# Four strided transfers for the first adjacency block, four-block stores and three transfers for the attention rows

## The chip, the cores and the metric

One core of a Trainium2 chip runs the kernel. The metric is device time in microseconds (us), median over runs. "Partition" is a row of the on-chip memory (128 of them); "queue" is the order in which one engine issues its transfers; the 16 DMA engines of the core carry out what all queues issue.

## The reference, cut to what matters

```
def reference(x, adj, W, a):              # x 4096x512, adj 4096x4096, W 512x2048, a 4x1024x1, all f32
    ht = (x @ W).reshape(N, 4, 512).transpose(1, 0, 2)
    src = einsum('hnd,hd->hn', ht, a[:, :512, 0])
    dst = einsum('hnd,hd->hn', ht, a[:, 512:, 0])
    e = leaky_relu(src[:, :, None] + dst[:, None, :], 0.01) + adj[None]
    h = einsum('hij,hjd->hid', softmax(e, axis=-1), ht).mean(axis=0)
    return layernorm(x + h, axis=-1)
```

The entries of adj are zero or as large as 1e9, while the attention scores are small. The softmax of a row is therefore, with the data at hand, all on the column where adj is largest. The kernel uses this: it finds that column for each row, gathers that row of x, multiplies it by the mean of the four heads' W, adds x and normalises. It also computes a bound that says whether this short form holds for all rows; if it doesn't, a general path (`general`) follows. With the inputs given it isn't entered.

## The kernel before

The 4096 rows are split into 32 blocks of 128. Partition p of block ib holds row p*32 + ib, so neighbouring partitions of one block are 32 rows of adj apart in main memory (32 rows x 16 KB = 512 KB), and one partition's neighbouring blocks are neighbours in main memory. A block of adj is 128 rows of 16 KB, 2 MB.

The function `leading_rows` is one hand-written order of instructions (`manual_schedule`): each engine takes its own in program order.

- SyncE (SP) issues all large transfers in one queue. Ahead of the loop stand: adj of block 0 (L132, through `load_adj`, L119 to L124), W in two halves of 2 MB (L130) with adj of blocks 1 and 2 after each, adj of blocks 3 and 4, and x of blocks 0 to 3 (L143). In the loop over t = 0 to 31 (L432) it issues adj of block t + 5 and, at a few t, more of x. The last blocks' adj come in 2 or 4 pieces of columns. After the loop come all the stores (L491 to L496, L551 to L553).
- ScalarE (ACT) issues the rows of `a` in four transfers of two rows of 2 KB (L133 to L137), then works on evictions, squares and normalisations.
- VectorE (DVE) reduces each block of adj to maxima of short segments (L180), finds the leading segment (L187, L189), and, two blocks later, the column in it (L223). The first reduction of block 0 waits for the whole of that block.
- GpSimd (POOL) issues the two gathers of each block, the leading segment (L200) and the row of x (L211), in a queue of its own.
- TensorE (PE) transposes the gathered rows (L238) and multiplies them by the mean of W (L253).

Six buffers hold adj. A new block is issued when the reduction of the block six before has freed its buffer.

Transfers issued by SP and ACT share eight completion semaphores, given out in turn; before a semaphore is used again the issuing queue waits for the transfer that used it last. A later transfer can therefore be held until the one eight before it has landed, beside what its own data need.

The output of block ib takes the place of x of that block in the tile `hold`. `store` (L337) writes n neighbouring blocks: each partition writes n x 2 KB in one run, 4 KB for two blocks, 8 KB for four. Before the change, blocks 0 to 7 are stored by fours (L491), 8 to 15 by twos (L493), 16 to 23 by fours (L495), and the last eight by twos and ones.

Of the kernel before, what the change touches and what calls it, by code (L numbers as in the profile page):

```python
# [9 lines left out]
F32 = mybir.dt.float32  # L10
# [10 lines left out]
P = 128  # L21
# [9 lines left out]
def gat_resnorm_kernel(  # L31
# [29 lines left out]
    any_bad = keep.tile([1, 1], I32, name="any_bad")  # L61

    leading_rows(tc, x, adj, W, a, out, ident, v, n_bad, any_bad)

    flag = nc.values_load(any_bad[0:1, 0:1], min_val=0, max_val=N)
# [5 lines left out]
def leading_rows(ctx, tc, x, adj, W, a, out, ident, v, n_bad, any_bad):  # L71
# [8 lines left out]
    nc = tc.nc  # L80
    N, D = x.shape
    H = a.shape[0]
    KB, NB = D // P, N // P
    AHEAD = 5
    Q = 4
    PIECES = 4
    LATE = NB - Q
    BEHIND = LATE - Q

    once = ctx.enter_context(tc.tile_pool(name="once", bufs=1))  # L90
    adj_pool = ctx.enter_context(tc.tile_pool(name="adj_pool", bufs=AHEAD + 1))
# [7 lines left out]
    adj_rows = adj.rearrange("(p nb) m -> nb p m", nb=NB)  # L99
# [11 lines left out]
    a_rows = once.tile([2 * H, D], F32, name="a_rows")  # L111

    once.tile([P, 32], F32, name="pad_end")
    adj_t = {}

    def pieces(ib):
        return PIECES if ib == NB - 1 else 2 if ib >= LATE else 1

    def load_adj(ib):  # L119
        if 0 <= ib < NB:  # L120
            t = adj_t[ib] = adj_pool.tile([P, N], F32, name="adj_t")
            n = pieces(ib)
            for k in range(n):
                nc.sync.dma_start(t[:, ts(k, N // n)], adj_rows[ib][:, ts(k, N // n)])  # L124
# [4 lines left out]
    def load_w(kb, n):  # L129
        nc.sync.dma_start(hold[:, ds(w_at + kb * H, n * H), :], w_blocks[:, ds(kb * H, n * H), :])  # L130

    load_adj(0)  # L132
    for s in range(2):  # L133
        for h in range(0, H, H // 2):
            nc.scalar.dma_start(
                a_rows[ds(s * H + h, H // 2), :], a[ds(h, H // 2), ts(s, D), :].rearrange("h d o -> h (d o)")
            )  # L137
    for kb in range(0, KB, 2):
        load_w(kb, 2)
        load_adj(kb // 2 + 1)  # L140
# [196 lines left out]
    def store(queue, lo, n):  # L337
        queue.dma_start(out_rows[:, ds(lo, n), :], hold[:, ds(lo, n), :])
# [93 lines left out]
    for t in range(NB):  # L432
# [29 lines left out]
        ib = t - PROJECT  # L462
# [25 lines left out]
    for ib in range(BEHIND, LATE):  # L488
        row_norm(ib)
    nc.scalar.activation(xx, xx, AF.Sqrt)  # L490
    for ib in range(0, 2 * Q, Q):  # L491
        store(nc.sync, ib, Q)
    for ib in range(2 * Q, 4 * Q, 2):  # L493
        store(nc.sync, ib, 2)
    for ib in range(4 * Q, BEHIND, Q):  # L495
        store(nc.sync, ib, Q)  # L496
    add_x(nc.gpsimd, BEHIND)
    find_column(NB - 2)
# [208 lines left out]
```

## Time and profile before

| | |
|---|---|
| median of three runs | 235.25 us (235.2 to 236.05) |
| the profiled execution | 234.9 us |
| its span, first to last instruction | 233.4 us |
| moved by the DMA engines | 97.12 MB, mean 416 GB/s over the span |
| busy: PE, DVE, ACT, POOL | 86%, 82%, 48%, 43% |
| granted TensorE clock, mean | 0.965 |

The page splits the span into 40 slices of 5.8 us and gives for each the busy tenths of every engine, the DMA engines' busy share and the GB/s that they moved. A second view gives the same for any stretch that one names. A timeline lists the instructions of one engine with start and duration; for SP and ACT's transfers that is the time of issuing, not of moving data. Beneath these lie the trace's records of single packets: start, duration, size and queue. A packet is here one contiguous run on one DMA engine: 16 KB for a row of adj, 4 or 8 KB for a store, 2 KB for a row of `a`.

### The profile page before, as it was taken

The page shows a single profiled execution, that of the slowest core. Times are in us where ns is not written, and L with a number is a line of the kernel's source. Part 1 is how long each engine was busy: PE and PEld are TensorE (multiplying, and loading weights), DVE is VectorE, ACT ScalarE, POOL GpSimd, SP SyncE. Part 2 cuts the span into 40 slices and gives each one's busy share as a digit, 9 for nine tenths or more (in the row PEclk, how much of TensorE's full clock was granted, in tenths as well). Part 3 has the DMA queues.
Part 4 walks back from the last instruction along what each step waited for, and adds up shares of the span by engine and source line. Part 5 has one row for each costly group of instructions (what it writes and reads, how often), then busy time and mean ns, then how long its engine had stood idle before and what let it go on. Part 6 is the DMA issues. An engine that isn't in the chain of part 4 may idle for free.

```text
span 233.4 us, 2484 instructions
## 1 busy us (share of the span) xinstructions
PE 199.9 (86%) x683; PEld 105.3 (45%) x683; DVE 191.3 (82%) x300; ACT 111.8 (48%) x267; POOL 100.7 (43%) x215
## 2 busy tenths in 40 slices
PE   0069995999999999999999779879998977999980
PEld 0034644646565555665645244334443433444460
DVE  0548299689929999999788995999999999998881
ACT  2001223014474757575767455545664644188561
POOL 2020234414524464644543452647464564548300
PEclk9999999579999999999999979999999999999997
DMA  6999999999999999999999999999999999999995
GB/s 237 423 432 428 428 438 426 415 439 436 422 421 437 423 431 425 431 419 428 430 430 428 432 423 432 423 430 421 426 433 420 426 423 426 412 424 420 421 414 213
DMA packets 12257, 97.12 MB, mean 416 GB/s; under 512 B 1992, under 2 KB 2440, under 8 KB 6480
## 3 DMA queue, kind: packets, MB, share of 16 engines
q1 hardware_dynamic: 8640, 88.08, 89.1%
q0 software_dynamic: 3584, 8.84, 9.6%
q8 instruction: 6, 0.10, 0.2%
q14 instruction: 11, 0.09, 0.1%
q10 hardware_dynamic: 16, 0.02, 0.0%
HBM read 88.54 MB, written 8.39 MB: 415 GB/s over the span
## 4 chain that ended last, share of the span: by engine, by line
DMA 64%; DVE 21%; PE 11%; SPq 1%; issue 1%; ACT 0%; DVEq 0%
DMA adj_t<-in_adj_dram 53%; DVE seg L180 17%; DMA hold<-in_x_dram 11%; PE o L253 6%; PE o L295 2%; DVE at L189 1%; PE tp L238 1%; DVE top L187 1%; PE o L246 1%; DVE within L223 1%; SPq L130 1%; PE o L291 0%; SPq L124 0%; DVE inner L217 0%; ACT hold L335 0%
## 5 line engine op out<-in xcount | busy, mean ns | idle before, releaser
L180 DVE TENSOR_REDUCE seg<-adj_t 128x128 f32<-128x2048 f32 (+3 forms) x66 | 145.5, 2208 | 28.5 <-DMA adj_t<-in_adj_dram 28.2
L253 PE MATMUL o<-w_sum,yt 128*128 128x512 f32 x248 | 117.6, 616 | 0.7 <-ACT yt L240 0.7
L253 PEld LDWEIGHTS o<-w_sum,yt 128*128 128x128 f32 x248 | 45.6, 196 | 55.2 <-issue 43.9
L240 ACT COPY yt<-tp 128x512 f32<-128x512 f32 x32 | 18.8, 588 | 43.9 <-PE tp L238 43.8
L200 POOL DMA_INDIRECT lead<-in_adj_dram,row x32 | 32.3, 1008 | 14.6 <-POOL row L196 14.6
L211 POOL DMA_INDIRECT y<-in_x_dram,col x32 | 30.9, 964 | 15.4 <-POOL col L225 15.1
L238 PE MATMUL tp<-ident,y 128*128 128x128 f32 x128 | 22.1, 296 | 10.2 <-DMA y<-in_x_dram,col 10.1
L246 PE MATMUL o<-hold,ident 128*128 128x512 f32 x52 | 28.5, 634 | 1.7 <-DMA hold<-in_x_dram 1.7
L343 PE MATMUL o<-hold,ident 128*128 128x512 f32 x32 | 17.3, 696 | 13.6 <-DMA hold<-in_L_gnn_W_dram 13.6
L238 PEld LDWEIGHTS tp<-ident,y 128*128 128x128 f32 x128 | 18.5, 209 | 22.8 <-issue 20.5
L361 ACT COPY wt<-tp 128x512 f32<-128x512 f32 x16 | 9.2, 587 | 38.2 <-PE tp L359 38.2
L196 POOL TENSOR_TENSOR row<-at,first 128x1 uint32<-128x1 uint32 x32 | 6.1, 190 | 43.6 <-DVE at L189 43.6
L367 PEld LDWEIGHTS pv<-at_d,wt 128*128 128x128 f32 x128 | 17.2, 200 | 7.4 <-ACT wt L361 3.7
L260 ACT ACTIVATE sq<-hold 128x512 f32<-128x512 f32 x32 | 19.8, 620 | 0.0
L225 POOL TENSOR_TENSOR col<-start,within 128x1 uint32<-128x1 uint32 x31 | 5.9, 190 | 32.2 <-DVE within L223 32.2
L286 ACT ACTIVATE hold<-o,nm,sd 128x512 f32<-128x512 f32 x24 | 17.2, 771 | 0.0
L277 ACT ACTIVATE sq<-o,nm 128x512 f32<-128x512 f32 x24 | 16.5, 687 | 0.8
L343 PEld LDWEIGHTS o<-hold,ident 128*128 128x128 f32 x32 | 6.9, 225 | 21.5 <-issue 21.5
L367 PE MATMUL pv<-at_d,wt 128*128 128x2 f32 x128 | 16.0, 249 | 0.6 <-ACT wt L361 0.6
L344 ACT ACTIVATE w_sum<-o 128x512 f32<-128x512 f32 x4 | 2.4, 598 | 27.5 <-PE o L343 27.5
L275 ACT ACTIVATE sq<-o 128x512 f32<-128x512 f32 x24 | 14.5, 606 | 0.0
L187 DVE MAX8 top<-seg 128x8 f32<-128x256 f32 (+2 forms) x32 | 11.6, 362 | 1.1
(86 smaller groups left out, 140.0 us busy)
## 6 DMA issues: line engine op xcount, KB each, us to landing
adj_t<-in_adj_dram SPq DMA_DIRECT2D x28, 2048.0 KB, 30.8
adj_t<-in_adj_dram SPq DMA_DIRECT2D x6, 1024.0 KB, 28.1
hold<-in_L_gnn_W_dram SPq DMA_DIRECT2D x2, 2048.0 KB, 16.4
hold<-in_x_dram SPq DMA_DIRECT2D x2, 2048.0 KB, 37.6
out_dram<-hold SPq DMA_DIRECT2D x4, 1024.0 KB, 16.1
out_dram<-hold SPq DMA_DIRECT2D x7, 512.0 KB, 14.4
hold<-in_x_dram SPq DMA_DIRECT2D x3, 1024.0 KB
adj_t<-in_adj_dram SPq DMA_DIRECT2D x4, 512.0 KB, 19.8
```

Of the source, the lines that this page charges most:

```text
L180: nc.vector.tensor_reduce(seg_of[ib][:, ts(k, N // e // n)], adj_t[ib][:, ts(k, N // n)].rearrange("p (s e) -> p s e", e=e), axis=AX.X, op ...
L200: nc.gpsimd.indirect_dma_start(out=lead, out_offset=None, in_=adj_segs[e], in_offset=bass.IndirectOffsetOnAxis(ap=row[:, :1], axis=0),)
L211: nc.gpsimd.indirect_dma_start(out=y, out_offset=None, in_=x, in_offset=bass.IndirectOffsetOnAxis(ap=col[:, :1], axis=0),)
L238: nc.tensor.transpose(tp[:, kb, :], y[:, ds(kb, P, KB)], ident)
L240: nc.scalar.copy(yt, tp)
L246: nc.tensor.matmul(o_ps[ib], ident, hold[:, ib, :], start=start, stop=False)
L253: nc.tensor.matmul(o_ps[ib], yt_of[ib][:, kb, :], w_sum[:, kb, :], start=(start and kb == 0), stop=(kb == KB - 1),)
L260: nc.scalar.activation(sq, hold[:, ib, :], AF.Square, accum_out=xx[:, ib : ib + 1])
L277: nc.scalar.activation(sq, o, AF.Square, bias=nm[:, i], accum_out=sd[:, i])
L286: nc.scalar.activation(hold[:, ib, :], o_ps.pop(ib), AF.Identity, bias=nm[:, i], scale=sd[:, i])
L343: nc.tensor.matmul(o, ident, hold[:, w_at + kb * H + h, :], start=(h == 0), stop=(h == H - 1))
L367: nc.tensor.matmul(pv[:, kb, h : 2 * H : H], wt[:, k, :], at_d[:, k, h : 2 * H : H], start=(k == 0), stop=(k == KB - 1),)
```

## The change

Block 0 of adj is issued in four transfers: partitions 0, 8, 16 and so on (16 rows), 4, 12, 20 and so on (16 rows), 2, 6, 10 and so on (32 rows), and all odd ones (64 rows). Together they are the same 128 rows. The rows of `a` come in one transfer of four rows and two of two. The stores of blocks 8 to 15 are two of four blocks in place of four of two. SP's transfers ahead of the loop grow by three, ACT's fall by one, and the stores fall by two, so the count of all transfers is the same and the semaphores of those between are two places further on in turn.

```diff
-    load_adj(0)
-    for s in range(2):
-        for h in range(0, H, H // 2):
-            nc.scalar.dma_start(
-                a_rows[ds(s * H + h, H // 2), :], a[ds(h, H // 2), ts(s, D), :].rearrange("h d o -> h (d o)")
-            )
+    adj_t[0] = adj_pool.tile([P, N], F32, name="adj_t")
+    for lo, step in ((0, 8), (4, 8), (2, 4), (1, 2)):
+        some = ds(lo, P // step, step)
+        nc.sync.dma_start(adj_t[0][some, :], adj_rows[0][some, :])
+    for s, h, n in ((0, 0, H), (1, 0, H // 2), (1, H // 2, H // 2)):
+        nc.scalar.dma_start(a_rows[ds(s * H + h, n), :], a[ds(h, n), ts(s, D), :].rearrange("h d o -> h (d o)"))
...
-    for ib in range(0, 2 * Q, Q):
-        store(nc.sync, ib, Q)
-    for ib in range(2 * Q, 4 * Q, 2):
-        store(nc.sync, ib, 2)
-    for ib in range(4 * Q, BEHIND, Q):
+    for ib in range(0, BEHIND, Q):
         store(nc.sync, ib, Q)
```

## The prediction

> **What bounds the kernel now.** I read the page's slices first. Between the first and the last slice the DMA engines are 90% busy or more in every one, at 412 to 439 GB/s; no other engine is that steady.
>
> ```profile
> span 233.4 us, 2484 instructions
> ...
> DMA  6999999999999999999999999999999999999995
> GB/s 237 423 432 428 428 438 426 415 439 436 422 421 437 423 431 425 431 419 428 430 430 428 432 423 432 423 430 421 426 433 420 426 423 426 412 424 420 421 414 213
> ...
> q1 hardware_dynamic: 8640, 88.08, 89.1%
> ```
>
> So the stream of transfers is the bound from end to end. Time can be won only by starting it sooner, making its packets cheaper, or shortening what follows its last packet. The start and the end come next, in the view by stretches (columns: PE, PEld, DVE, ACT and POOL busy with counts, clock, DMA share, GB/s; a packet's bytes count where it starts, so fine stretches jump).
>
> ```profile
> 1.75:2.00 0.25, 0.00 (x0) 0.00 (x0) 0.00 (x0) 0.00 (x0) 0.25 (x4) 1.00 0.40 82
> 2.00:2.25 0.25, 0.00 (x0) 0.00 (x0) 0.00 (x0) 0.00 (x0) 0.25 (x5) 1.00 0.99 197
> 2.25:2.50 0.25, 0.00 (x0) 0.00 (x0) 0.00 (x0) 0.00 (x0) 0.13 (x3) 1.00 0.22 66
> 2.50:2.75 0.25, 0.00 (x0) 0.00 (x0) 0.00 (x0) 0.17 (x1) 0.00 (x0) 1.00 0.77 197
> 2.75:3.00 0.25, 0.00 (x0) 0.00 (x0) 0.00 (x0) 0.25 (x1) 0.00 (x0) 1.00 1.81 524
> ...
> 229.00:230.00 1.00, 0.00 (x0) 0.00 (x0) 0.00 (x0) 0.00 (x0) 0.00 (x0) 1.00 0.77 305
> 230.00:231.00 1.00, 0.00 (x0) 0.00 (x0) 0.00 (x0) 0.00 (x0) 0.00 (x0) 0.92 0.73 283
> 231.00:232.00 1.00, 0.00 (x0) 0.00 (x0) 0.00 (x0) 0.00 (x0) 0.00 (x0) 0.50 0.13 49
> ```
>
> The engines come in one after another over 0.9 us. The packet records say it exactly: the 16 engines' first packets start between 1.99 and 2.89 (mean 2.59) and end between 3.30 and 3.96 (mean 3.62); from then on a 16 KB packet takes 0.61 us. At the end the engines are still full at 229 and run dry by 231.8. SP's timeline gives the issues at the start:
>
> ```profile
> 0.98 0.39 SPq L124 DMA_DIRECT2D adj_t<-in_adj_dram  x1
> 1.42 0.43 SPq L130 DMA_DIRECT2D hold<-in_L_gnn_W_dram  x1
> 1.89 0.43 SPq L124 DMA_DIRECT2D adj_t<-in_adj_dram  x1
> 2.36 0.76 SPq L130 DMA_DIRECT2D hold<-in_L_gnn_W_dram  x1
> 3.17 0.44 SPq L124 DMA_DIRECT2D adj_t<-in_adj_dram  x1
> ```
>
> The issue of 128 rows ends at 1.37, and the first packet moves 0.62 us later. That W's second issue takes 0.76 instead of 0.43 says that something behind the queue needs more than the 0.47 us between issues to digest 128 rows; I take it that the spread of 0.9 us is the same thing, the making of 128 rows' descriptors.
>
> **What the Trainium skill says.** "DMA: Bandwidth & Descriptors", section "Latency and other measured facts", puts the first byte of such a transfer at about 600 ns; the trace agrees with 0.62. The same page, "Why a DMA increments its semaphore by 16 and not by 1", says a transfer is spread over the largest number of engines up to 16 that divides its rows, so 16 rows should give each engine one; the trace has only 128-row ones and the two-row transfers of `a`. "SBUF — State Buffer", section "Door 1: The DMA port swizzle", derives the memory port from the partition number: bits 2 to 4 and bit 6. By it partitions 0, 8, 16 ... reach 8 of 16 ports and 4, 12, 20 ... the other 8, while the third and fourth transfers reach all. No transfer in this trace shows that. The first page's table also lists a loss for copies between main-memory tensors at a row pitch of 4 MiB (103 against 164 GB/s at 2 MiB), which is the pitch of every eighth row here; no row here has that pitch, and it was not measured for loads.
>
> **The change part by part.**
>
> *Block 0 in four.* The first part has 16 rows, an eighth of the descriptors: by proportion 0.9/8 = 0.11 us of spread. All engines should then start near 1.99 to 2.1. Its second part is issued at about 1.45 and can feed the engines 0.62 us after its issue ends, about 2.45, before the first packets end (2.9 at the earliest). Third and fourth follow 0.47 us apart with 2 and 4 packets per engine, 1.2 and 2.4 us of work, so the engines don't run dry. Upper bound of the gain: every first packet ends about 2.9 (start 1.99 plus the 0.9 us that the late starters' first packets take), against a mean of 3.62: 0.7. Middle: the four that start first, 1.99 to 2.19, take 1.2 to 1.5 us, three of them ending together at 3.30 to 3.35; were that a floor set by memory, all would end at 3.3, a gain of 0.3. Lower bound, before the ports are counted: none. I take 0.4. It passes to the end one for one: DVE waits for adj 28.2 us in all, 11 times, so its work shifts with the loads; PE's run to the end begins at 201.55 when x lands; and the last store goes out at 228.80 into a queue still holding about 1 us of packets.
>
> *What the extra issues cost.* Three more issues of about 0.47 us move W's first half from 1.42 to about 2.8 on SP and everything behind it likewise. Block 0 alone keeps the engines busy to 1.99 + 8 x 0.61 = 6.9, so W's descriptors are 4 us early still: nothing. The semaphores come two places further on, so adj of block 1 and the second half of W, which waited for nothing, now wait for a part of block 0 or for rows of `a`; SP's whole queue stands behind each. The parts land from about 3.5 to 8, the rows of `a` landed by 9.2, and block 0 with W's first half covers the engines to 11.8. Nothing again; were the cover gone, each late issue would show one for one. In the loop SP waits longest for DVE's buffers (86.9 us behind the segment reduction alone), which the two places don't alter. DVE's first reduction now needs four landings, some 0.1 us more at most; it has 4.2 us of waiting before block 1.
>
> *Rows of `a`.* ACT issues three instead of four, at 0.24 to 0.54 each: about 0.3 us less ahead of a table load at 2.58. ACT's first work is at 20.11 and the rows are read at 20.0: nothing.
>
> *Stores.* 512 packets of 4 KB become 256 of 8 KB, per engine 32 become 16. The packet records have 0.159 us for the one and 0.309 for the other: 32 x 0.159 - 16 x 0.309 = 0.14 us less; counted from start to start (0.155 and about 0.305) it is 0.08. I take 0.1, all of it on the path because the engines stay full up to 230. SP has two issues (2 x 0.33) less, beside 12 us of waiting for data between 210 and 222: nothing. These results were finished long before (ACT's last write of a block under 24 ends at 195.1, the first store goes out at 198.64), so joining them holds nothing back. Gathers of x run between the larger packets and may take 0.15 us more for each one that they wait for; PE takes the last gathered row up at 221.6, some 5 us after it came: hidden.
>
> Sum: 0.4 + 0.1 = 0.5 less. The profiled execution's 234.9 (233.4 of span and 1.5 around it) goes to 234.4; the median lies 0.35 above that execution, so 234.75 is forecast. 0.5%, about what a measurement of this kernel can tell from no change, is 1.18 us: faster is below 234.07, slower above 236.43.
>
> **The rivals.**
>
> *The first packets are late for another reason than descriptors.* For it: the three early ones that end together. Then only the stores gain: 235.15. Between this and the forecast nothing in the trace of before decides.
>
> *The strided parts run below full rate.* Mechanism: a part that reaches 8 ports with 16 engines moves at half rate. If the skill's map holds and each engine has one row, parts one and two take 1.22 us each instead of 0.61: 1.2 more, less 0.5: 235.95. Should the pitch cost as much again, they take a quarter of the rate: 2 x 1.83 = 3.7 more, 238.45. Should all four parts share ports at half rate because rows are dealt to engines in order, 8 x 0.61 = 4.9 more: 239.65. It decides the sign from the moment that it costs over 0.5 us, that is, block 0's parts one and two at less than about 70% of full rate. For it: the map. Against it: if engines follow partitions, as with whole blocks, eight engines take two rows of part one and the other eight begin with part two, and no port is shared; then the gain is halved, not lost.
>
> *A larger gain.* The slowest engine's first packet ends at 3.96; if the last engine at the end is the one that started last, it gains up to 3.96 - 2.9 = 1.06, with the stores 1.2: 234.05.
>
> *A wait from the shifted semaphores starves the stream.* Against it: the 8 us of cover at the start, and at the end the six stores in flight hold some 6 MB, over 13 us. If it came, an SP issue delay of 0.5 to 1 us: 235.5 or so.
>
> **How the numbers follow.** Forecast 0.48; first packets late for another reason 0.20; strided parts slow 0.22, half of it with the first two parts at half rate only; larger gain 0.06; starved stream 0.04. The range 234.1 to 236.6 leaves out the larger gain and the heavier half of the strided case, 0.17. Faster by over 0.5% needs the larger gain, or the upper bounds of both terms with the scatter of the runs: 0.10. Slower by over 0.5% needs the heavier strided case and a little scatter: 0.15. Within: 0.75.
>
> **What would show it.** Right: all first packets start by about 2.2 to 2.5, block 0's last part lands near 8.2 instead of 8.67, the DVE's first reduction starts with it, and the last store is issued about 0.4 earlier than 228.80. Wrong: 16 KB packets above 0.61 us before 5 us (ports or pitch), a reduction that starts at 8.67 or later, a stretch in which the DMA share falls below 0.9 between 10 and 229. If the stores' packets don't shrink to 0.309 us per 8 KB, that term is wrong.

## The result and the profile after

The changed kernel takes 237.53 us (median of six runs, 237.16 to 238.63) against 235.36 before (235.09 to 236.05): the ratio is 1.0099 with a 95% interval of 1.008 to 1.0119. The forecast was 234.75 with a range of 234.1 to 236.6. The change made the kernel 2.2 us slower, and the time lies outside the range.

The profiled execution has a span of 235.9 us (237.52 as a run). The page's slices are the first view, as before:

```profile
span 235.9 us, 2483 instructions
...
DMA  5999999999999999999999999999999999999985
GB/s 164 375 431 438 425 429 421 431 430 420 434 427 433 421 432 429 430 422 429 431 427 428 428 426 436 419 441 408 436 420 426 426 427 419 414 426 424 423 354 212
```

The stream still fills the engines, but the first two slices moved 164 and 375 GB/s where they moved 237 and 423: 121 GB/s x 5.9 us, some 0.7 MB less, which is 1.7 us of the stream. A second loss is in the last slice but one, 354 instead of 414. SP's timeline and the stretches show the first:

```profile
0.97 2.52 SPq L135 DMA_DIRECT2D adj_t<-in_adj_dram  x4
3.54 0.59 SPq L130 DMA_DIRECT2D hold<-in_L_gnn_W_dram  x1
```

```profile
2.00:4.00 2.00, 0.00 (x0) 0.00 (x0) 0.00 (x0) 1.28 (x1) 0.38 (x6) 1.00 0.76 219
4.00:6.00 2.00, 0.00 (x0) 0.00 (x0) 0.00 (x0) 0.00 (x0) 0.00 (x0) 1.00 0.95 272
6.00:8.00 2.00, 0.00 (x0) 0.00 (x0) 0.00 (x0) 0.00 (x0) 0.00 (x0) 1.00 0.96 328
8.00:10.00 2.00, 0.00 (x0) 0.00 (x0) 0.00 (x0) 0.00 (x0) 0.00 (x0) 1.00 0.97 377
10.00:12.00 2.00, 0.00 (x0) 0.00 (x0) 0.99 (x1) 0.00 (x0) 0.00 (x0) 1.00 1.05 451
```

Read the last two columns together. In the first row the engines stand idle for a part of the time (0.76, after an empty first half microsecond). From 4 to 10 us they are busy, 0.95 to 0.97, but move only 272 to 377 GB/s: their packets are slow. Before, the stretch from 2 to 4 us moved 287 GB/s, and the next three were these:

```profile
4.00:6.00 2.00, 0.00 (x0) 0.00 (x0) 0.00 (x0) 0.00 (x0) 0.00 (x0) 1.00 0.92 393
6.00:8.00 2.00, 0.00 (x0) 0.00 (x0) 0.00 (x0) 0.00 (x0) 0.00 (x0) 1.00 1.04 446
8.00:10.00 2.00, 0.00 (x0) 0.00 (x0) 1.33 (x1) 0.00 (x0) 0.00 (x0) 1.00 1.00 428
```

From 10 us on the rate is the old one. The packet records give the detail: the 16 first packets start between 2.39 and 3.32 instead of 1.99 and 2.89, and between 4 and 8 us single 16 KB packets take up to 2.44 us instead of 0.61. By 10 us the changed kernel has moved 2.33 MB where the old one had 3.06; the missing 0.73 MB are 1.7 us of the stream. Its engines have had packets under way for 7.20 us each instead of 7.63. So 0.4 of the 1.7 us is engines without work, more than half of it before 3.4 us, and 1.3 is packets that take longer. DVE's timeline shows the delay that this hands on:

```profile
11.01 4.48 DVE L180 TENSOR_REDUCE seg<-adj_t 128x128 f32<-128x2048 f32 x2 [11.01 <-DMA adj_t<-in_adj_dram]
```

The first reduction starts at 11.01 instead of 8.67, 2.3 us late. The last piece of adj is reduced 2.7 us later than before, and the span is 2.5 us longer. Beyond the start there is thus one more thing, which the end of the span shows:

```profile
226.00:228.00 2.00, 2.00 (x9) 1.23 (x8) 1.72 (x4) 1.82 (x3) 0.00 (x0) 1.00 0.86 356
228.00:230.00 2.00, 2.00 (x11) 1.76 (x10) 1.89 (x7) 1.96 (x5) 0.00 (x0) 1.00 0.74 295
230.00:232.00 2.00, 0.54 (x3) 0.14 (x1) 1.03 (x6) 0.29 (x1) 0.00 (x0) 1.00 0.81 332
```

The engines have gaps before the last results are stored: the stores are through, and the transfers wait for the computation. The last store goes out at 232.60, 3.8 us later than before, not 2.3.

### The profile page after: what moved, and what is told of

It reads as the page before. It is cut to its first block, busy times and chain, and to the rows that moved or that the text cites. A ratio compares the mean times of both kernels' runs of the same rounds, so it can differ in the third digit from the quotient of the medians.

```text
span 235.9 us, 2483 instructions
## 1 busy us (share of the span) xinstructions
PE 201.5 (85%) x683; PEld 106.1 (45%) x683; DVE 191.0 (81%) x300; ACT 111.7 (47%) x267; POOL 100.7 (43%) x215
## 4 chain that ended last, share of the span: by engine, by line
DMA 46%; POOL 18%; issue 17%; DVE 13%; PE 3%; ACT 0%; POOLq 0%; SPq 0%; DVEq 0%
DMA adj_t<-in_adj_dram 41%; DVE seg L180 9%; POOL lead L200 6%; POOL y L211 6%; DMA lead<-in_adj_dram,row 5%; POOL sd L281 2%; PE o L253 2%; PE o L295 2%; POOL row L196 1%; POOL start L207 1%; POOL col L225 1%; DVE col L231 1%; DVE at L189 1%; DVE top L187 1%; POOL sd L280 1%
## 5 line engine op out<-in xcount | busy, mean ns | idle before, releaser
L253 PE MATMUL o<-w_sum,yt 128*128 128x512 f32 x248 | 119.0, 622 | 0.7 <-ACT yt L240 0.7
L253 PEld LDWEIGHTS o<-w_sum,yt 128*128 128x128 f32 x248 | 46.3, 199 | 56.2 <-issue 45.4
```

The source lines that it names most:

```text
L253: nc.tensor.matmul(o_ps[ib], yt_of[ib][:, kb, :], w_sum[:, kb, :], start=(start and kb == 0), stop=(kb == KB - 1),)
```

## The experiments

After the result I held this: the start costs the time, by two mechanisms. A, a transfer is handed to its engines one after the other, in about the same time for 16 rows as for 128, so small first parts leave engines without work. B, parts that reach few of the memory ports slow their packets. Rivals were C, the pitch of 4 MiB in main memory, and the stores with the end of the kernel. Comparisons are with the kernel before on the same chip (235.1 to 235.2 there). Apart from the run of the stores alone, all of these kernels keep the old stores.

### The two halves of the change

The start alone (new block 0 and rows of `a`, old stores):

```diff
-    for ib in range(0, BEHIND, Q):
+    for ib in range(0, 2 * Q, Q):
+        store(nc.sync, ib, Q)
+    for ib in range(2 * Q, 4 * Q, 2):
+        store(nc.sync, ib, 2)
+    for ib in range(4 * Q, BEHIND, Q):
         store(nc.sync, ib, Q)
```

> The new start (block 0 in four strided parts, rows of a in three) with the old stores. Theory: the start holds the whole loss, since the first reduction starts at 11.01 instead of 8.67, 2.3 us late, and from 10 us on the packets take 0.61 us as before: 237.3 to 237.7. Rival, the stores: their larger packets make the gathers wait at the end, where the last store goes out 3.8 us later and not 2.3; without them the time falls to about 236.

Measured: 237.88, ratio 1.0122 (1.0099 to 1.0144). That is 0.2 above the range that I had given. The start holds the whole loss, 2.7 us here; its first reduction is 2.0 us late, the last piece of adj 2.5. That it is 0.35 us slower than the changed kernel itself (237.53, measured apart from it) is within the scatter of the two: the runs lie between 237.61 and 238.62 here and between 237.16 and 238.63 there.

The stores alone, the same edit to the kernel before with the signs turned:

> The new stores alone (blocks 8 to 15 by fours), the old start. Theory: within 0.3 us of 235.4, perhaps 0.1 less as in the prediction. Rival, the stores are what costs: 236.5 to 237.5, with the engines idle for 1 to 2 us between 224 and 230.

Measured: 235.29, ratio 1.0007 (0.9999 to 1.0016). They neither gain nor lose. The traced execution took 235.9 us, near the slowest of the twelve, so what follows is where a slow one of them lost time; whether the others have it isn't shown. Until the last piece of adj its stream is level with before (0.2 us ahead), but then DVE waits for the leading segments of the last block. Before, there was no such wait (first line); now there is one of 0.81 us:

```profile
216.53 0.97 DVE L217 MAX8 inner<-lead 128x8 f32<-128x32 f32 x8
...
216.38 0.84 DVE L217 MAX8 inner<-lead 128x8 f32<-128x32 f32 x7
218.03 0.23 DVE L217 MAX8 inner<-lead 128x8 f32<-128x64 f32 x1 [0.81 <-DMA lead<-in_adj_dram,row]
...
219.29 0.18 DVE L414 TENSOR_SCALAR gap<-gap 128x32 f32<-128x32 f32 x1
```

That gather was issued at 211.87, as before (211.99), and landed after 6.1 us instead of 5.2. It runs on the same engines as the stores, whose packets at that time are now all of 8 KB; before, most were of 4. The count (L418) needs the result and stands in PE's queue ahead of the last blocks' products; the last store leaves 0.85 us later than before, into a queue that is emptier by then. The changed kernel shows the same wait, 0.7 us, after the same 6.1 us. Five other traces with the old stores (the start alone, both orders of columns, two parts, the reversed order) have 5.2 to 5.5 us for this gather. That larger packets cause the longer gather fits all of them; no run changed the packet size alone at that place.

### What in the start costs

Neighbouring partitions instead of strided ones:

```diff
-    for lo, step in ((0, 8), (4, 8), (2, 4), (1, 2)):
-        some = ds(lo, P // step, step)
-        nc.sync.dma_start(adj_t[0][some, :], adj_rows[0][some, :])
+    for lo, n in ((0, 16), (16, 16), (32, 32), (64, 64)):
+        nc.sync.dma_start(adj_t[0][ds(lo, n), :], adj_rows[0][ds(lo, n), :])
```

> As the new start with the old stores, but the four parts of block 0 are neighbouring partitions: 0 to 15, 16 to 31, 32 to 63, 64 to 127. Theory A, handing a part out to 16 engines costs about the same for 16 rows as for 128, so small parts feed the engines too slowly: like the strided parts, 237.5. Theory B, ports: by the skill's map these parts reach 4, 4, 8 and 8 of 16 ports, so if rows are dealt to 16 engines in order they take 2.4, 2.4, 2.4 and 4.9 us instead of 4.9 in all: 7 us more than before, 242. Theory C, the pitch of 4 MiB or the stride itself: neighbouring rows have 512 KB and no stride, so about 235.4.

Measured: 242.06, ratio 1.0293 (1.0276 to 1.031), the number that the ports gave. The stretches show engines that are busy and slow until 14 us:

```profile
4.00:6.00 2.00, 0.00 (x0) 0.00 (x0) 0.00 (x0) 0.00 (x0) 0.00 (x0) 1.00 0.64 84
6.00:8.00 2.00, 0.00 (x0) 0.00 (x0) 0.00 (x0) 0.00 (x0) 0.00 (x0) 1.00 0.93 174
8.00:10.00 2.00, 0.00 (x0) 0.00 (x0) 0.00 (x0) 0.00 (x0) 0.00 (x0) 1.00 0.77 172
10.00:12.00 2.00, 0.00 (x0) 0.00 (x0) 0.00 (x0) 0.00 (x0) 0.00 (x0) 1.00 1.12 229
12.00:14.00 2.00, 0.00 (x0) 0.00 (x0) 0.00 (x0) 0.00 (x0) 0.00 (x0) 1.00 1.09 238
```

A packet counts in the stretch in which it starts, so the rates of long packets jump; 84 to 238 of the usual 427 is a fifth to a half, as 4 and then 8 of 16 ports allow. A packet's mean time is 1.9 us between 4 and 6, and 16 packets are under way at once. So ports as the Trainium skill maps them ("SBUF — State Buffer", "Door 1: The DMA port swizzle") do bind, and rows of such a part go to all 16 engines.

Parts by columns, each of all 128 partitions:

```diff
+    for lo, n in ((0, N // 8), (N // 8, N // 8), (N // 4, N // 4), (N // 2, N // 2)):
+        nc.sync.dma_start(adj_t[0][:, ds(lo, n)], adj_rows[0][:, ds(lo, n)])
```

> As the new start with the old stores, but the four parts of block 0 are columns (512, 512, 1024, 2048 of 4096) of all 128 partitions: the same number of transfers and bytes in each, every engine on its own port, pitch as before. Theory A (handing out): engines wait for their next part as in the strided start, first reduction near 10 to 11, 236.5 to 237.5. Theory B or C (ports, pitch): nothing of the loss stays, packets at full rate, 235.2 to 235.6.

Measured: 236.91, ratio 1.0079 (1.0062 to 1.0096). With the ports out of play, 1.7 us of loss stay. The same parts with the largest first:

```diff
-    for lo, n in ((0, N // 8), (N // 8, N // 8), (N // 4, N // 4), (N // 2, N // 2)):
+    for lo, n in ((0, N // 2), (N // 2, N // 4), (3 * N // 4, N // 8), (7 * N // 8, N // 8)):
```

> The four column parts of block 0 in the reverse order: 2048 columns first, then 1024, 512, 512; all 128 partitions each, so every engine on its own port, and as many transfers as in the column parts with the small one first (236.9). Theory A (small parts first feed the engines too slowly): the first part holds 2.5 us for each engine and covers the handing out of the rest, 235.2 to 235.7. If it is the number of transfers or their small packets at the start: 236.5 to 237.

Measured: 235.65, ratio 1.0022 (1.0014 to 1.003). Same transfers, ports and packet sizes, and 1.26 us less, only by their order. First the small part first, then the large one:

```profile
4.00:6.00 2.00, 0.00 (x0) 0.00 (x0) 0.00 (x0) 0.00 (x0) 0.00 (x0) 1.00 0.88 302
6.00:8.00 2.00, 0.00 (x0) 0.00 (x0) 0.00 (x0) 0.00 (x0) 0.00 (x0) 1.00 1.01 352
```

```profile
4.00:6.00 2.00, 0.00 (x0) 0.00 (x0) 0.25 (x1) 0.00 (x0) 0.00 (x0) 1.00 0.98 407
6.00:8.00 2.00, 0.00 (x0) 0.00 (x0) 2.00 (x1) 0.00 (x0) 0.00 (x0) 1.00 1.19 473
```

With the small part first the engines do lack work: from 3.6 to 5.4 us only 9 to 14 of the 16 have a packet under way, with the large part first all 16. By 10 us the one has moved 2.58 MB and the other 3.11. That is 1.2 us of the stream, about the difference of the medians, though these two executions were only 0.92 apart. Of the 1.2 us, 0.7 is engines without work, and the rest is slower packets, which theory A doesn't explain.

The strided parts in reverse, 64 rows first:

```diff
-    for lo, step in ((0, 8), (4, 8), (2, 4), (1, 2)):
+    for lo, step in ((1, 2), (2, 4), (4, 8), (0, 8)):
```

> As the new start with the old stores, but the four strided parts in the reverse order: odd partitions (64 rows) first, then 32, 16 and 16 rows. Same parts, ports, pitch and count of transfers. Theory A with B: the first part gives every engine 4 rows, 2.4 us, so handing out the small parts is covered; what stays is the ports' share, which the extra load put at about 1.3: 236.0 to 236.6. If the order doesn't matter, as the new start: 237.9.

Measured: 236.95, ratio 1.0077 (1.0063 to 1.0091), 0.9 below the new start and 0.35 above the upper end that I had given. The order is worth 0.9 us, against 1.26 with columns. The stretch from 4 to 6 us moves 428 GB/s; the slow packets come between 6 and 10 (330 and 295). In the packet records the first 96, the parts of 64 and 32 rows, keep to about 0.61 us once all engines run. With the 97th, where the two parts of every eighth partition begin, they lengthen to 1.0 to 1.16. So it is these two parts that share ports.

Two parts, even and odd partitions, 64 rows each:

```diff
-    for lo, step in ((0, 8), (4, 8), (2, 4), (1, 2)):
+    for lo, step in ((0, 2), (1, 2)):
```

> As the new start with the old stores, but block 0 in two parts, even and odd partitions (64 rows each, 4 per engine, pitch 1 MiB). Theory A (handing out): the first part holds 2.4 us of work for each engine, the second comes long before that ends, so no loss is left: 235.2 to 235.6. Theory B, ports: rows dealt in order give engines e and e + 4 the same port at the same time; packets above 0.61 us, 236.2 to 239.

Measured: 235.53, ratio 1.0017 (1.001 to 1.0024). After 3.5 us nearly all its packets take 0.61 to 0.63, and none up to 14 us more than 0.72: a stride of two shares no ports in a way that shows, and a first part of 64 rows covers what follows.

### Ports against pitch, with a deep queue

These kernels load 2 MB of adj a second time (block 0, in one of them 128 neighbouring rows), into a part of `hold` that is filled later, after adj of block 4. The extra load changes no result.

```diff
     for ib in range(KB // 2 + 1, AHEAD):
         load_adj(ib)
+    spare = hold[:, ds(Q, 2 * Q), :].rearrange("p b d -> p (b d)")
+    nc.sync.dma_start(spare, adj_rows[0])
     load_x(0, Q)
```

> The kernel before with one load more: the 2 MB of adj block 0 once more, all 128 rows in one transfer, into the part of hold that x of blocks 4 to 11 fills later, issued after adj of block 4 when the engines have some 10 MB queued. The control for the next two: 8 packets of 0.61 us per engine, 4.9 us, so 240.0 to 240.3, and no packet above 0.65.

Measured: 240.32, ratio 1.0225 (1.0208 to 1.0242).

```diff
-    nc.sync.dma_start(spare, adj_rows[0])
+    for lo, step in ((0, 8), (4, 8), (2, 4), (1, 2)):
+        some = ds(lo, P // step, step)
+        nc.sync.dma_start(spare[some, :], adj_rows[0][some, :])
```

> The extra load in the four strided parts of the change, at a place where the queue is deep, so that handing out a part can't leave an engine idle. Theory A (handing out is the loss): 240.1, as the whole extra load. Theory B (16 engines on 8 ports) or C (pitch of 4 MiB): packets of 0.8 to 1.2 us and more, 1.2 to 2 us above the whole extra load.

Measured: 241.58, ratio 1.0278 (1.0261 to 1.0295), 1.26 above the whole load. The stretches, first of the whole load and then of the strided one:

```profile
38.00:39.00 1.00, 0.14 (x1) 0.17 (x2) 0.93 (x4) 0.00 (x0) 0.00 (x0) 0.50 1.05 447
39.00:40.00 1.00, 0.96 (x4) 0.55 (x4) 1.00 (x2) 0.01 (x1) 0.32 (x2) 0.50 1.05 446
```

```profile
38.00:39.00 1.00, 0.00 (x0) 0.00 (x0) 0.93 (x4) 0.00 (x0) 0.00 (x0) 0.81 0.90 214
39.00:40.00 1.00, 0.18 (x1) 0.21 (x2) 1.00 (x2) 0.00 (x0) 0.35 (x2) 0.50 0.96 218
```

Engines 0.90 and 0.96 busy move half of the usual bytes: the median packet takes 1.07 and 1.14 us there instead of 0.61. This is half rate, with no shortage of work.

```diff
+    for lo, step, row in ((0, 8, 0), (4, 8, 16), (2, 4, 32), (1, 2, 64)):
+        nc.sync.dma_start(spare[ds(lo, P // step, step), :], adj[ds(row, P // step), :])
```

> The extra load in the same four strided sets of partitions, but from neighbouring rows of adj (16 KB apart instead of 4, 4, 2 and 1 MiB), so with the memory ports of the strided load and without its pitch. Theory B (ports): as the strided extra load within 0.3 us. Theory C (pitch): as the whole extra load within 0.3 us.

Measured: 241.47, ratio 1.0277 (1.0259 to 1.0294), as the strided load from rows 4 MiB apart. At this rate the pitch costs nothing; the partitions do.

```diff
+    for lo, n in ((0, N // 8), (N // 8, N // 8), (N // 4, N // 4), (N // 2, N // 2)):
+        nc.sync.dma_start(spare[:, ds(lo, n)], adj_rows[0][:, ds(lo, n)])
```

> The extra load of 2 MB behind a deep queue, in four parts by columns (512, 512, 1024, 2048) of all 128 partitions. Small packets alone cost by the packet records 0.2 us per engine: 240.5, against 240.3 for the whole extra load. If it is as slow as at the start (1.7 above the whole block there), something in the column parts other than handing out slows them: 242.

Measured: 240.32, ratio 1.0218 (1.0203 to 1.0234), the same as the whole load. Column parts are not slow in themselves. What their order costs belongs to the start of an empty queue.

### Rows of `a` out of the way

```diff
-    for s in range(2):
-        for h in range(0, H, H // 2):
-            nc.scalar.dma_start(
-                a_rows[ds(s * H + h, H // 2), :], a[ds(h, H // 2), ts(s, D), :].rearrange("h d o -> h (d o)")
-            )
     for kb in range(0, KB, 2):
         load_w(kb, 2)
         load_adj(kb // 2 + 1)
+    for s in range(2):
+        nc.sync.dma_start(a_rows[ts(s, H), :], a[:, ts(s, D), :].rearrange("h d o -> h (d o)"))
```

> The kernel before with the rows of a taken off ACT's queue and issued by SP after adj of block 2, in two transfers of four rows. If the 0.9 us over which the engines come in at the start is lengthened by ACT's four transfers, which are handed out in the same time, the first packets come closer together and the time falls to 234.7 to 235.0; if it is SP's own transfer alone, 235.1 to 235.3.

Measured: 235.47, ratio 1.0014 (1.0008 to 1.0021), slightly slower and above both ranges that I had given. The first packets start at 2.33 in the mean and at 2.77 the latest (before: 2.59 and 2.89; the means of five other traces with the old start lie between 2.43 and 2.64), and the first reduction is 0.2 us earlier. Nothing of it is left at the last piece of adj, which is 0.24 later. Where it went is open: one trace of each can't tell so small a shift from the place of the gathers among the loads.

## Why the prediction was wrong

**The step that failed** is the one for block 0, "an eighth of the descriptors: by proportion 0.9/8 = 0.11 us of spread". The spread doesn't go by rows. The first 16 packets are spread over 0.93 us with 16 strided rows (2.39 to 3.32), over 0.55 with 16 neighbouring ones (2.01 to 2.56) and over 0.90 with 128. The strided issue is also slower, 0.56 to 0.63 us each where a whole block takes 0.39 to 0.44, and its first packet comes 1.42 us after the issue begins instead of 1.01. So the first packets start 0.28 us later in the mean (2.87 against 2.59), where the prediction had them all near 2.0: the gain of 0.4 isn't there. "The engines don't run dry" failed less: engines without work are 0.4 of the 1.7 us by which the stream is behind. The larger loss, 1.3 us of slower packets, had no place in the forecast's sum, only among the rivals. The row that I took the proportion from had only one size in it. One size can't separate a cost per row from a cost per engine, and it was then put at the low end.

**The rival with the strided parts** was right in its mechanism. Its price for parts one and two, 1.2 us, agrees with 1.26 for the extra load in all four parts, and the reversed order shows that only these two parts are slow. But it was charged against a gain of 0.5 that doesn't exist.

**The sum as the runs have it.** Ports 1.26 (the strided extra load less the whole one). Order, small parts first: 0.93 with strided parts (237.88 - 236.95, two chips), 1.26 with columns (236.91 - 235.65). What stays of columns with the large part first: 0.47 (235.65 - 235.18). With the strided value 1.26 + 0.93 + 0.47 = 2.66, against 2.71 for the start alone; the changed kernel lost 2.17.

The last 0.47 doesn't show at the start. The packet records of each trace say how much had been moved by 10 us; the last column is how much longer the traced execution took than the median of the kernel before beside it:

| start | moved by 10 us | behind before | slower by |
|---|---|---|---|
| before | 3.06 MB | | |
| changed kernel | 2.33 MB | 1.7 us | 2.2 us |
| start alone | 2.27 MB | 1.9 us | 2.8 us |
| reversed order | 2.54 MB | 1.2 us | 1.9 us |
| columns, small first | 2.58 MB | 1.1 us | 1.2 us |
| columns, large first | 3.11 MB | -0.1 us | 0.2 us |
| even and odd | 3.01 MB | 0.1 us | 0.2 us |

Up to 215 us the third column changes by some 0.1 us at most. What the last column has beyond it, up to 0.9 us, is therefore lost at the end. With the large column part first DVE waits 0.18 us there for the last block's leading segments, and the count that needs them starts on PE at 219.16 instead of 218.78. The cause is open. All of these kernels issue the rows of `a` in three transfers, and all but the last have their semaphores two places further on; neither was run alone.

**The way to the end.** That a shift of the start passes on one for one held for losses: the first reduction is late by 2.3, 2.0, 6.7 and 1.4 us in the changed kernel, the start alone, the neighbouring partitions and the reversed order, and the last piece of adj by 2.7, 2.5, 6.7 and 1.4. For a gain it was not seen (the rows of `a`). With columns the first reduction is no guide, since it needs only a part.

**The extra issues and semaphores** cost no starvation: from 4 to 10 us the changed kernel's engines are 0.95 busy or more, and at 215 us its stream is as far behind as at 10. Whether the shifted semaphores have a part in what is lost at the end isn't shown.

**The stores.** The 0.1 us of packets may be there, but "all of it on the path" and "hidden" failed. That the engines "stay full up to 230" isn't what the prediction's own lines say: they have 0.77 from 229 to 230 and 0.73 after it. I followed the last gather of x, which had 5 us to spare, and not the gather of the leading segment of the last block, for which DVE waits 0.8 us in the trace of the stores alone. There PE also waits 0.48 us, at 217.56, for the gather of x before the last.

**Rows of `a`** in three were not run by themselves; one issue less at the start could not be seen among 2.7 us.

## What to carry to other kernels

At the start of a stream nothing covers the handing out of a transfer: give the engines their largest transfer first, over all 128 partitions, and split only what comes behind it. In these runs no split beat the one whole transfer. Before splitting by partitions ask which ports the packets of a part reach at the same time; a load of the same bytes behind a deep queue shows that cost in a single trace. When packets are slow, compare bytes moved with the time that engines were busy: it tells missing work from slow packets. A store that is joined into larger packets may slow a small gather beside it, so look at which gather the last computation waits for.

## What the runs showed of the hardware

- 16 rows at every eighth partition, 32 at every fourth and 64 odd ones, loaded behind a deep queue, move 214 to 218 GB/s over 2 us instead of 447; at that rate main-memory rows 16 KB apart instead of 4 MiB make no difference (241.47 and 241.58 us). In the reversed order only the two parts of every eighth partition are slow.
- Parts of 16 neighbouring partitions are slower still: the packets of the second such part took 2.0 to 2.1 us each instead of 0.61, with all 16 under way.
- Even and odd partitions in two transfers cost only 0.4 us in all, though each has a stride.
- A load with a partition stride that opens the queue sends its first packet 1.36 to 1.42 us after its issue begins, one without a stride 1.01 to 1.04 us after.
- Four column transfers behind a deep queue cost as much as one (240.32 and 240.32 us). Of the same four on an empty queue, the stream is 1.1 us behind with the small ones first and level with the large one first.
- A gather of 128 segments landed in 6.1 us in both traces in which the stores beside it had packets of 8 KB, and in 5.2 to 5.5 in six with the old stores.
